# Layer 0 of a two-layer image kernel: gates made with tanh and spread over the slots, and a context that lags behind the attention

## The chip, the cores and the metric

The kernel runs on one core of one Trainium2 chip. The metric is the device time of one execution in microseconds (us), the median of several executions. A core has five engines that each work through their own list of instructions in order and meet at semaphores: TensorE (PE, with PEld for its weight loads), VectorE (DVE), ScalarE (ACT), GpSimd (POOL) and SyncE (SP), which here only issues DMA transfers.

## The reference, cut to what matters

Layer 0 is linear attention on eight images of 128 x 128 points and 128 channels; layer 1 is a selective scan on its output. Layer 0, and the part of layer 1 that this kernel computes together with it:

```python
q, k, v = split(x @ w_qkv)                     # 4 heads of 32
q = softmax(q over the 32 of a head) * 32**-0.5
k = softmax(k over all 16384 points)
context = einsum('bhdn,bhen->bhde', k, v)
out = (context applied to q) @ w_out + b_out
x1 = layernorm(out) * gamma + beta + x         # layer 0's output
xz = x1 @ Win;  xb, z = split(xz)              # layer 1 begins
zf = silu(z)                                   # "the gates", used at the very end of layer 1
```

## The kernel before, in words

The program is three parts one after the other: `layer0`, `layer1_front` and `layer1_scan`. Only `layer0` is touched.

**Tiling.** An image lies in SBUF channel by channel as `xs[b % 2]` (`x` in the profile), 128 partitions by 16384 points, so two images are held at a time. It is worked in 32 groups of 512 points (`NG`, `GN`). Images are taken in the order `ORDER`; `b` below is the place in that order, 0 to 7.

**Stages of one group.** Context: `key` (matmul `pk`, copy to `k`), `larger` (running maximum over four groups, folded to 128 columns), `fold` (transpose `pmt`, maximum `m` per partition, the scale `a`, a diagonal `dg`), `spread` (the maximum to all partitions, `pmx`), `value` (`pv`, copied to `vt`), `subtract` and `raise_to` (exponential), `add` (four matmuls into `pc`). Attention: `query` (matmul `pq`, maximum `qm`, difference `q`, both on DVE), `exponent` (exp on ACT), `normalize` (sum, reciprocal, product on POOL), `through_wo` (four matmuls `pg`, copy `gt` on ACT), `through_context` (matmul `po`, bias `o` on DVE, square `sq` on ACT), `variance` (DVE), `scale` (three POOL operations that end in `d`), `turn` (four matmuls `pt`), `finish` (`x1t` on ACT, the sum back into `x` on POOL, and for half of the images the store of x1). Gates: `gate_group` makes `z` of a finished group: for some images a copy `v` of the group in the other order of points (DVE, line 152; it is also what is stored as x1 for `ORDER[b] < 4`), then for each of two channel halves a matmul `pz` (line 161), Silu on ACT (line 163) and a store to `zs`.

**Loops.** `image(b)` runs slots `t`. In a slot the attention of image b takes group t (its later stages take t-1, t-2, t-3), and the context of image b+1 takes group `a = t - later` with `later = 1`, its `value` and exponential five groups behind, its `add` six. An image has 39 slots; the first call, `b = -1`, has only a context. The gates of image b-1 are all made in slot 0 of image b, 32 groups in a row, and then image b+1 is loaded over the buffer of image b-1. The last image has no context; there two gate groups are made in each slot, one of image 6 and one of image 7.

**What sets the order.** The code is written slot by slot and `in_order` pins every engine to the order in which the code issues: an instruction that waits holds all that stand behind it on its engine. PSUM tiles of the tag `ps` rotate through six banks, so a matmul waits until the sixth tile before its own has been read. SP issues the DMAs in program order.

```python
for t in range(later + NG + BK + 2):
    a = t - later
    ...
    at(through_wo, t - 1)
    ...
    at(exponent, t)
```

Of the kernel before, what the change touches and what calls it, by code (L numbers as in the profile page):

```python
# [8 lines left out]
F32 = mybir.dt.float32  # L9
BF16 = mybir.dt.bfloat16  # L10
AF = mybir.ActivationFunctionType
ALU = mybir.AluOpType
AX = mybir.AxisListType
# [3 lines left out]
P = 128  # L17
B = 8
# [3 lines left out]
NC2 = 2  # L22
R = 8
K = 4
GW = 4
GN = GW * H
NG = W // GW
BK = 4
ORDER = (0, 1, 4, 5, 2, 3, 6, 7)
LATER = 1  # L30
CH = 1024
CW = CH // H
NCH = L // CH
# [44 lines left out]
def layer0(ctx: ExitStack, tc, xT, w_qkv, w_out, b_out, gamma, beta, win, x1, zs):  # L78
# [12 lines left out]
    nc = tc.nc  # L91
    const = ctx.enter_context(tc.tile_pool(name="l0c", bufs=1))
    wp = ctx.enter_context(tc.tile_pool(name="l0w", bufs=2))
    sm = ctx.enter_context(tc.tile_pool(name="l0s", bufs=4))
    ps = ctx.enter_context(tc.tile_pool(name="l0p", bufs=6, space=PSUM))
    psc = ctx.enter_context(tc.tile_pool(name="l0pc", bufs=1, space=PSUM))

    ident = const.tile([P, P], F32, name="ident")
# [7 lines left out]
    nc.sync.dma_start(wq, w_qkv)  # L106
    wz = const.tile([P, NC2 * P], F32, name="wz")
    nc.sync.dma_start(wz, win[:, NC2 * P :])
    wo = const.tile([P, P], F32, name="wo")
    nc.sync.dma_start(wo, w_out)  # L110
    bb = const.tile([P, GW, P], F32, name="bb")
# [13 lines left out]
    xs = [const.tile([P, W, H], F32, name=f"x{i}") for i in range(2)]  # L125
# [13 lines left out]
    def group(b, g):  # L139
        return xs[b % 2][:, g * GW : (g + 1) * GW, :]  # L140

    def load(b, pieces=range(8)):
        for i in pieces:
            s = slice(16 * i, 16 * i + 16)
            nc.sync.dma_start(xs[b % 2][:, s, :], xT[ORDER[b], :, s, :])

    def gate_group(b, g):

        v = group(b, g)
        if ORDER[b] % K < 2 or ORDER[b] < B // 2:  # L150
            t = wp.tile([P, GW, P], F32, name="v", bufs=4)
            nc.vector.tensor_copy(
                t, xs[b % 2].rearrange("p w h -> p h w")[:, g * GW : (g + 1) * GW, :]
            )
            if ORDER[b] < B // 2:
                nc.sync.dma_start(x1[ORDER[b]][:, g * GN : g * GN + GN], t.rearrange("p w h -> p (w h)"))
            if ORDER[b] % K < 2:
                v = t
        for c in range(NC2):
            pz = ps.tile([P, GW, P], F32, name="pz", tag="ps")  # L160
            nc.tensor.matmul(pz, wz[:, c * P : c * P + P], v, start=True, stop=True)
            z = wp.tile([P, GW, P], F32, name="z", tag="k", bufs=7)
            nc.scalar.activation(z, pz, AF.Silu)
            dst = zs[ORDER[b], c][:, g * GN : g * GN + GN]
            nc.sync.dma_start(dst, z.rearrange("p w h -> p (w h)"))

    def gate(b):

        for g in range(NG):
            gate_group(b, g)  # L170
        if b + 2 < B:
            load(b + 2)

    def context(b):

        ks, pks, ms, runs, scales = {}, {}, {}, {}, {}

        def key(g):
            pk = ps.tile([P, GW, P], F32, name="pk", tag="ps")
            nc.tensor.matmul(pk, wq[:, P : 2 * P], group(b, g), start=True, stop=True)  # L180
            ks[g] = k = wp.tile([P, GW, P], F32, name="k", tag="k", bufs=7)
            nc.scalar.copy(k, pk)
            pks[g] = pk

        def larger(g):
            pk = pks.pop(g)
            j, i = divmod(g, BK)
            if i == 1:
                runs[j] = run = wp.tile([P, GW, P], F32, name="run")
                nc.vector.tensor_tensor(run, pk, ks[g - 1], ALU.max)  # L190
            elif i > 1:
                nc.vector.tensor_tensor(runs[j], pk, runs[j], ALU.max)

            if i == BK - 1:
                run = runs[j]
                nc.vector.tensor_tensor(run[:, 0:2], run[:, 0:2], run[:, 2:4], ALU.max)
                nc.vector.tensor_tensor(run[:, 0], run[:, 0], run[:, 1], ALU.max)

        def fold(g):

            j, i = divmod(g, BK)
            if i < BK - 1:
                return
            run = runs.pop(j)
            turned = ps.tile([P, P], F32, name="pmt", tag="ps")
            nc.tensor.transpose(turned, run[:, 0, :], ident)
            ms[j] = m = sm.tile([P, 1], F32, name="m")
            nc.vector.tensor_reduce(m, turned, AX.X, ALU.max)
            if j:
                nc.vector.tensor_tensor(m, m, ms[j - 1], ALU.max)  # L210
                scales[j] = a = sm.tile([P, 1], F32, name="a")
                nc.vector.tensor_tensor(a, ms.pop(j - 1), m, ALU.subtract)
            runs[j] = dg = sm.tile([P, P], F32, name="dg", bufs=2)
            nc.vector.tensor_scalar(dg, ident, m, None, ALU.mult)

        def spread(g):
            j, i = divmod(g, BK)
            if i == BK - 1:
                nc.tensor.matmul(pm[:, j % 2, :], ones, runs.pop(j), start=True, stop=True)
                if j:  # L220
                    nc.scalar.activation(scales[j], scales[j], AF.Exp)

        def value(g):
            pv = ps.tile([P, GW, P], F32, name="pv", tag="ps")
            nc.tensor.matmul(pv, wq[:, 2 * P : 3 * P], group(b, g), start=True, stop=True)
            nc.scalar.copy(vts[g % 3][:, :, 0:P], pv)

        def subtract(g):

            mb = pm[:, g // BK % 2 : g // BK % 2 + 1, :]  # L230
            nc.vector.tensor_tensor(ks[g], ks[g], mb.to_broadcast([P, GW, P]), ALU.subtract)

        def raise_to(g):
            nc.scalar.activation(ks[g], ks[g], AF.Exp)

        def add(g):
            k = ks.pop(g)
            j, n = divmod(g, BK)
            for i in range(GW):
                nc.tensor.matmul(  # L240
                    pc, k[:, i, :], vts[g % 3][:, i, :],
                    start=(n == 0 and i == 0), stop=(n == BK - 1 and i == GW - 1),
                )
            if n < BK - 1:
                return
            if j:
                nc.vector.scalar_tensor_tensor(total, total, scales.pop(j), pc, ALU.mult, ALU.add)
            else:
                nc.vector.tensor_copy(total, pc)
            if g == NG - 1:  # L250
                rs = sm.tile([P, 1], F32, name="rs")
                nc.vector.reciprocal(rs, total[:, P : P + 1])
                for h in range(NH):
                    s = slice(HD * h, HD * h + HD)
                    nc.vector.tensor_scalar(
                        ctxs[b % 2][s, s], total[s, s], rs[s, :], HD**-0.5, ALU.mult, ALU.mult
                    )

        return key, larger, fold, spread, value, subtract, raise_to, add

    def attend(b):
# [69 lines left out]

        return query, exponent, normalize, through_wo, through_context, variance, scale, turn, finish

    def image(b):

        key = larger = fold = spread = value = subtract = raise_to = add = None
        query = exponent = normalize = through_wo = through_context = None
        variance = scale = turn = finish = None
        later = LATER if b >= 0 else 0
        if b + 1 < B:  # L340
            key, larger, fold, spread, value, subtract, raise_to, add = context(b + 1)
        if b >= 0:
            (query, exponent, normalize, through_wo, through_context, variance, scale, turn,
             finish) = attend(b)

        def at(stage, g):
            if stage is not None and 0 <= g < NG:
                stage(g)

        for t in range(later + NG + BK + 2):  # L350
            a = t - later
            at(scale, t - 2)
            at(finish, t - 3)
            at(query, t)
            if b == B - 1 and t < NG:
                gate_group(b - 1, t)
            at(through_wo, t - 1)
            if b == B - 1 and 4 <= t < NG + 4:
                gate_group(b, t - 4)
            at(exponent, t)  # L360
            at(subtract, a - BK - 1)
            at(raise_to, a - BK - 1)
            at(key, a)
            at(normalize, t)
            at(fold, a - 1)
            at(value, a - BK - 1)
            at(larger, a)
            at(through_context, t - 1)
            at(add, a - BK - 2)
            at(turn, t - 2)  # L370
            at(spread, a - 1)
            at(variance, t - 1)
            if t == 0 and 0 < b < B - 1:
                gate(b - 1)

    with in_order(tc):
        load(0)
# [892 lines left out]
```

## Time and profile before

| | us |
|---|---|
| median of 3 runs (9255.66 to 9263.38) | 9257.32 |
| the profiled execution | 9261.02 |
| its span | 9259.2 |
| layer 0 ends (the first instruction of the next part) | 2388 |
| first query matmul of images 0 to 7 | 109, 336, 634, 933, 1221, 1507, 1804, 2098 |

The span of the profiled execution is 1.8 us shorter than its time. Of its 9259.2 us layer 0 takes the first 2388, in which TensorE is busy about 90% of the time; from there on VectorE and GpSimd are the full engines. In the profile a float32 matmul shows as two instructions, so the 256 query matmuls are counted as 512. "Idle before, releaser" tells how long an engine stood still ahead of an instruction, and what it waited for.

### The profile page before, as it was taken

The page shows a single profiled execution, that of the slowest core. Times are in us where ns is not written, and L with a number is a line of the kernel's source. Part 1 is how long each engine was busy: PE and PEld are TensorE (multiplying, and loading weights), DVE is VectorE, ACT ScalarE, POOL GpSimd, SP SyncE. Part 2 cuts the span into 40 slices and gives each one's busy share as a digit, 9 for nine tenths or more (in the row PEclk, how much of TensorE's full clock was granted, in tenths as well). Part 3 has the DMA queues.
Part 4 walks back from the last instruction along what each step waited for, and adds up shares of the span by engine and source line. Part 5 has one row for each costly group of instructions (what it writes and reads, how often), then busy time and mean ns, then how long its engine had stood idle before and what let it go on. Part 6 is the DMA issues. An engine that isn't in the chain of part 4 may idle for free. (4 is left out here: it accounts for less than half of the span.)

```text
span 9259.2 us, 91316 instructions
## 1 busy us (share of the span) xinstructions
PE 6337.5 (68%) x24512; PEld 3096.6 (33%) x24512; DVE 7992.0 (86%) x7953; ACT 7099.7 (77%) x8066; POOL 7316.5 (79%) x4684
## 2 busy tenths in 40 slices
PE   8899998988899999999434636446364463643636
PEld 5555555554333333333101304114031140311403
DVE  6667666774699999999799999999999999999996
ACT  5555555657789999999688887887878888888885
POOL 3446444554588988888599899998999989999897
PEclk9999999999999999999655757557575575755857
DMA  1322333123478789888758769587695876957767
GB/s 76 146 84 96 137 121 146 70 109 137 148 242 249 251 246 244 245 246 241 206 154 238 208 185 258 158 230 216 179 260 159 222 225 178 257 165 218 230 174 211
DMA packets 934769, 1750.66 MB, mean 189 GB/s; under 512 B 150228, under 2 KB 376148, under 8 KB 926064
## 3 DMA queue, kind: packets, MB, share of 16 engines
q1 hardware_dynamic: 873328, 1509.92, 49.4%
q0 software_dynamic: 60928, 234.90, 13.8%
q8 instruction: 200, 3.28, 0.1%
q14 instruction: 313, 2.56, 0.1%
HBM read 1052.36 MB, written 692.12 MB: 188 GB/s over the span
## 5 line engine op out<-in xcount | busy, mean ns | idle before, releaser
L951 POOL TENSOR_TENSOR h<-ubt,sp 128x1024 f32<-128x1024 f32 x1024 | 2422.4, 2399 | 348.4 <-ACT mv L1058 124.1
L934 PE MATMUL px<-rows,dtw 128*128 128x512 bf16 x2048 | 953.5, 565 | 2266.2 <-DVE y L1001 1084.5
L534 DVE SCALAR_TENSOR_TENSOR acc<-xb,cw,acc 128x1024 f32<-128x1024 f32 x1024 | 1320.3, 1289 | 133.7 <-ACT xb L502 89.9
L526 POOL TENSOR_TENSOR tap<-tap 128x1024 f32<-128x1024 f32 x512 | 1224.0, 2394 | 243.9 <-ACT tap L524 220.6
L938 ACT ACTIVATE sp<-px 128x1024 f32<-128x1024 f32 x1024 | 1047.3, 1024 | 435.4 <-PE px L934 418.1
L961 DVE TENSOR_TENSOR_SCAN h<-px,h 128x1024 f32<-128x1024 f32 x512 | 1177.3, 2331 | 31.7 <-ACT px L942 15.1
L934 PEld LDWEIGHTS <-dtw 128*128 128x128 bf16 x2048 | 169.1, 110 | 3089.1 <-issue 1022.7
L959 DVE TENSOR_TENSOR_SCAN h<-px,h 128x1024 f32<-128x1024 f32 x512 | 1177.9, 2330 | 21.4 <-POOL h L951 18.8
L1009 POOL TENSOR_TENSOR y<-y,h 128x512 f32<-128x512 f32 x768 | 1159.8, 1559 | 3.8 <-DVE h L982 3.8
L942 ACT ACTIVATE px<-sp,sa 128x1024 f32<-128x1024 f32 x1024 | 1110.4, 1109 | 6.1
L515 PE MATMUL acc<-xi,wt 128*128 128x512 f32 x2048 | 938.3, 601 | 53.7 <-ACT ures L539 53.7
L524 ACT ACTIVATE tap<-xb,cw 128x1024 f32<-128x1024 f32 x768 | 837.3, 1139 | 15.2 <-POOL xb L499 15.1
L282 POOL TENSOR_TENSOR q<-q,qs 128x512 f32<-128x512 f32 x256 | 272.2, 1063 | 695.5 <-DVE qs L281 695.5
L938 ACT ACT_TABLE_LOAD x512 | 656.9, 1283 | 170.0 <-PE px L934 168.0
L942 ACT ACT_TABLE_LOAD x512 | 656.9, 1283 | 9.1
L1074 PEld LDWEIGHTS px<-wg,z 128*128 128x128 f32 x4096 | 575.3, 225 | 114.8 <-issue 109.1
L1074 PE MATMUL px<-wg,z 128*128 128x128 f32 x4096 | 574.7, 308 | 0.0
L967 PE MATMUL pc<-rows,csel 128*128 128x512 bf16 x1024 | 517.5, 586 | 78.2 <-DVE rstd L1062 74.5
L515 PEld LDWEIGHTS acc<-xi,wt 128*128 128x128 f32 x2048 | 375.1, 189 | 574.4 <-issue 411.9
L488 PE MATMUL pxb<-xi,wi 128*128 128x512 f32 x1024 | 496.2, 607 | 2.1 <-ACT xb L497 2.1
L298 ACT ACTIVATE sq<-o 128x512 f32<-128x512 f32 x256 | 161.2, 630 | 421.0 <-DVE o L296 419.8
L1001 DVE TENSOR_TENSOR y<-y,px 128x1024 f32<-128x1024 f32 x384 | 468.6, 1220 | 14.4
(153 smaller groups left out, 15038.8 us busy)
## 6 DMA issues: line engine op xcount, KB each, us to landing
ubt<-ubs SPq DMA_DIRECT2D x1024, 512.0 KB
zs<-z SPq DMA_DIRECT2D x512, 256.0 KB
ubs<-ures SPq DMA_DIRECT2D x256, 512.0 KB
ubs<-turned SPq DMA_DIRECT2D x256, 512.0 KB
z<-zs SPq DMA_DIRECT2D x256, 512.0 KB
y<-gs POOLq DMA_DIRECT2D x128, 1024.0 KB, 10.3
gs<-du POOLq DMA_DIRECT2D x96, 1024.0 KB, 8.6
rows<-xps SPq DMA_DIRECT2D x1536, 60.0 KB
```

The costliest lines, as they stand in the source:

```text
L515: nc.tensor.matmul(acc[:, s, :], wt[:, j, c, :], x, start=(j == 0), stop=(j == len(ON_PE) - 1))
L524: nc.scalar.activation(t, at(n, c, *d), AF.Copy, scale=weight(n, c, *d))
L526: nc.gpsimd.tensor_tensor(sums[n, c], sums[n, c], t, ALU.add)
L534: nc.vector.scalar_tensor_tensor(acc, at(n, c, *d), weight(n, c, *d), acc, ALU.mult, ALU.add)
L934: nc.tensor.matmul(p[:, hf * 512 : hf * 512 + 512], sl.dw[:, c * P : c * P + P], src, start=True, stop=True)
L938: nc.scalar.activation(t, da[n, c], AF.Softplus)
L942: nc.scalar.activation(da[n, c], sp[n, c], AF.Exp, scale=sa[:, sl.s, c : c + 1])
L951: nc.gpsimd.tensor_tensor(h, u, t, ALU.mult)
L959: nc.vector.tensor_tensor_scan(e[:, ::-1], x[:, ::-1], e[:, ::-1], start, ALU.mult, ALU.add)
L961: nc.vector.tensor_tensor_scan(e, x, e, start, ALU.mult, ALU.add)
L1009: nc.gpsimd.tensor_tensor(v[:, c], v[:, c], h[:, c], ALU.add)
L1074: nc.tensor.matmul(po[:, w, :], z[:, c, w * H : w * H + H], wg[:, c, :], start=(c == 0), stop=(c == NC2 - 1))
```

## The change

Gates: Silu is made as half of z times (tanh of half of z, plus one). The weights `wz` are halved once at the start; ACT makes the tanh from PSUM, DVE forms (tanh + 1) times the PSUM tile with one instruction, and the store follows. `gate_group` falls into four stages, `ready` (the copy `v`, now on ACT), `gate_project`, `gate_tanh` and `gate_store`. They are no longer made in one go: a table `plan` gives each slot its gate groups. At the start of image b the gates of image b-1 that are still open are made two to a slot; from slot 35 on, when image b's attention has ended, its own gates are made one to a slot. `ready` runs one slot ahead, at the end of a slot.

Context: it starts when the open gates are done and `LEAD = 2` slots more have passed (`laters[b]`, 1 for image 0 and then 16, 9, 12, 11, 11, 11), so that an image has 39, 54, 47, 50, 49, 49 and 49 slots, and 37 for the last. The load of image b+1 is issued when the last gate of image b-1 has been issued.

Order in the slot: `exponent` comes ahead of `through_wo`; it stood behind it. Fold of maxima: one `tensor_reduce` instead of two `tensor_tensor` maxima; `m` and `a` are made with a scalar operand per partition instead of a second tensor.

```diff
+    nc.vector.tensor_scalar(wz, wz, 0.5, None, ALU.mult)
...
-            nc.vector.tensor_copy(
-                t, xs[b % 2].rearrange("p w h -> p h w")[:, g * GW : (g + 1) * GW, :]
-            )
+            nc.scalar.copy(t, xs[b % 2].rearrange("p w h -> p h w")[:, g * GW : (g + 1) * GW, :])
...
-            z = wp.tile([P, GW, P], F32, name="z", tag="k", bufs=7)
-            nc.scalar.activation(z, pz, AF.Silu)
...
+    def gate_tanh(b, g, c):
+        zts[b, g, c] = z = wp.tile([P, GW, P], F32, name="z", bufs=4)
+        nc.scalar.activation(z, pzs[b, g, c], AF.Tanh)
+
+    def gate_store(b, g, c):
+
+        z = zts.pop((b, g, c))
+        nc.vector.scalar_tensor_tensor(z, z, 1.0, pzs.pop((b, g, c)), ALU.add, ALU.mult)
+        nc.sync.dma_start(zs[ORDER[b], c][:, g * GN : g * GN + GN], z.rearrange("p w h -> p (w h)"))
...
-                nc.vector.tensor_tensor(run[:, 0:2], run[:, 0:2], run[:, 2:4], ALU.max)
-                nc.vector.tensor_tensor(run[:, 0], run[:, 0], run[:, 1], ALU.max)
+                runs[j] = top = sm.tile([P, P], F32, name="top", bufs=2)
+                nc.vector.tensor_reduce(top, run.rearrange("p w h -> p h w"), AX.X, ALU.max)
...
-                nc.vector.tensor_tensor(m, m, ms[j - 1], ALU.max)
+                nc.vector.tensor_scalar(m, m, ms[j - 1], None, ALU.max)
...
-                nc.vector.tensor_tensor(a, ms.pop(j - 1), m, ALU.subtract)
+                nc.vector.tensor_scalar(a, ms.pop(j - 1), m, None, ALU.subtract)
...
+    for b in range(-1, B):
+        left = NG - done[b - 1] if b > 0 else 0
+        if b >= 0:
+            laters[b] = -(-left // 2) + LEAD if left else 1
+        for t in range(laters[b] + NG + BK + 2 if b < B - 1 else NG + 5):
+            gates = plan[b, t] = []
+            for _ in range(2 if b < B - 1 else 1):
+                if b > 0 and done[b - 1] < NG:
+                    gates.append((b - 1, done[b - 1]))
+                    done[b - 1] += 1
+                    if done[b - 1] == NG and b + 1 < B:
+                        loads[b, t] = b + 1
+            if b < B - 1:
+                own = b >= 0 and not gates and t > NG + 2
+            else:
+                own = done[b] <= t - 5
+            if own and done[b] < NG:
+                gates.append((b, done[b]))
+                done[b] += 1
...
-        for t in range(later + NG + BK + 2):
-            a = t - later
+        for t in (t for i, t in times if i == b):
+            a = t - laters[b]
+            first, second = (plan[b, t] + [None, None])[:2]
             at(scale, t - 2)
             at(finish, t - 3)
             at(query, t)
-            if b == B - 1 and t < NG:
-                gate_group(b - 1, t)
+            if first:
+                gate_project(*first)
+                gate_tanh(*first, 0)
+            at(exponent, t)
+            if first:
+                gate_tanh(*first, 1)
+                gate_store(*first, 0)
             at(through_wo, t - 1)
-            if b == B - 1 and 4 <= t < NG + 4:
-                gate_group(b, t - 4)
-            at(exponent, t)
+            if second:
+                gate_project(*second)
             at(subtract, a - BK - 1)
             at(raise_to, a - BK - 1)
             at(key, a)
             at(normalize, t)
+            if first:
+                gate_store(*first, 1)
+            if second:
+                for c in range(NC2):
+                    gate_tanh(*second, c)
             at(fold, a - 1)
             at(value, a - BK - 1)
             at(larger, a)
             at(through_context, t - 1)
+            if second:
+                for c in range(NC2):
+                    gate_store(*second, c)
             at(add, a - BK - 2)
             at(turn, t - 2)
             at(spread, a - 1)
             at(variance, t - 1)
-            if t == 0 and 0 < b < B - 1:
-                gate(b - 1)
+            for g in plan.get(then.get((b, t)), ()):
+                ready(*g)
+            if (b, t) in loads:
+                load(loads[b, t])
```

More of the change, by code (lines that the diff above doesn't have):

```diff
@@ L29 @@
 ORDER = (0, 1, 4, 5, 2, 3, 6, 7)
-LATER = 1
+LEAD = 2
 CH = 1024
@@ L145, in load, with ready @@
             nc.sync.dma_start(xs[b % 2][:, s, :], xT[ORDER[b], :, s, :])
-    def gate_group(b, g):
+    vs, pzs, zts = {}, {}, {}
+    def ready(b, g):
         v = group(b, g)
@@ L158, in gate_group, with gate_project @@
                 v = t
+        vs[b, g] = v
+    def gate_project(b, g):
+        v = vs.pop((b, g))
         for c in range(NC2):
-            pz = ps.tile([P, GW, P], F32, name="pz", tag="ps")
+            pzs[b, g, c] = pz = ps.tile([P, GW, P], F32, name="pz", tag="ps")
             nc.tensor.matmul(pz, wz[:, c * P : c * P + P], v, start=True, stop=True)
-            z = wp.tile([P, GW, P], F32, name="z", tag="k", bufs=7)
[L163 to L172, printed above, removed]
+    def gate_tanh(b, g, c):
[5 more added lines that the diff above has]
+        nc.sync.dma_start(zs[ORDER[b], c][:, g * GN : g * GN + GN], z.rearrange("p w h -> p (w h)"))
     def context(b):
@@ L180, in key @@
             nc.tensor.matmul(pk, wq[:, P : 2 * P], group(b, g), start=True, stop=True)
-            ks[g] = k = wp.tile([P, GW, P], F32, name="k", tag="k", bufs=7)
+            ks[g] = k = wp.tile([P, GW, P], F32, name="k", bufs=7)
             nc.scalar.copy(k, pk)
@@ L203, in fold @@
                 return
-            run = runs.pop(j)
+            top = runs.pop(j)
             turned = ps.tile([P, P], F32, name="pmt", tag="ps")
-            nc.tensor.transpose(turned, run[:, 0, :], ident)
+            nc.tensor.transpose(turned, top, ident)
             ms[j] = m = sm.tile([P, 1], F32, name="m")
@@ L332, in attend @@
         return query, exponent, normalize, through_wo, through_context, variance, scale, turn, finish
+    plan, laters, loads = {}, {-1: 0}, {}
+    done = [0] * B
+    for b in range(-1, B):
[17 more added lines that the diff above has]
+                done[b] += 1
+    assert done == [NG] * B
+    times = list(plan)
+    then = dict(zip(times, times[1:]))
     def image(b):
@@ L338, in image @@
         variance = scale = turn = finish = None
-        later = LATER if b >= 0 else 0
         if b + 1 < B:
```

## The prediction

> **What bounds the kernel now.** I first took the windows, busy time per engine in stretches of 50 us (columns: window, length, PE, PEld, DVE, ACT, POOL busy with counts, granted clock, DMA share, GB/s).
>
> ```profile
> 200.00:250.00 50.00, 47.96 (x250) 32.60 (x248) 42.10 (x73) 31.13 (x55) 35.66 (x39) 1.00 0.00 1
> 350.00:400.00 50.00, 48.29 (x104) 18.06 (x102) 17.94 (x25) 31.02 (x52) 0.00 (x0) 1.00 1.01 382
> 2200.00:2250.00 50.00, 42.98 (x165) 22.88 (x166) 19.81 (x35) 40.15 (x58) 25.10 (x28) 1.00 0.42 158
> ```
>
> TensorE is full while attention and context run together (first line), full and DMA-bound in the gate run of slot 0 (second), less full in the last image (third). Then the timeline of one slot (start, duration, engine, line):
>
> ```profile
> 204.12 1.02 PE L268 MATMUL pq<-x,wq 128*128 128x512 f32 x2
> 204.98 1.05 PE L288 MATMUL pg<-wo,q 128*128 128x128 f32 x8
> 205.87 1.02 PE L180 MATMUL pk<-x,wq 128*128 128x512 f32 x2
> 206.73 1.02 PE L225 MATMUL pv<-x,wq 128*128 128x512 f32 x2
> 207.59 1.02 PE L294 MATMUL po<-gt,ctxn 128*128 128x512 f32 x2
> ...
> 210.23 1.02 PE L268 MATMUL pq<-x,wq 128*128 128x512 f32 x2
> ...
> 206.25 0.69 DVE L272 TENSOR_TENSOR q<-pq,qm 128x512 f32<-128x512 f32 x1
> ...
> 206.12 0.59 ACT L290 COPY gt<-pg 128x512 f32<-128x512 f32 x1 [0.62 <-PE pg L288]
> 206.98 0.63 ACT L275 ACTIVATE q<-q 128x512 f32<-128x512 f32 x1 [0.27 <-DVE q L272]
> ```
>
> Matmul groups follow at 0.86 (four-fold ones 0.89), seven make 6.11, and po stands 3.47 after pq. gt comes before the exponential; keep that in mind. Every fourth slot (fold) takes 7.82: VectorE is held there, as the group view over 130:2100 (POOL at work) and over 20:100 (POOL idle) says:
>
> ```profile
> L212 DVE TENSOR_TENSOR a<-m 128x1 f32<-128x1 f32 x49 | 41.9, 854 | 1.7
> L212 DVE TENSOR_TENSOR a<-m 128x1 f32<-128x1 f32 x6 | 1.0, 159 | 0.2
> ```
>
> Image boundary, the last slot of the layer, and the rows for the changed operations (ACT's only strided copy of 512 elements is layer 1's `turned`):
>
> ```profile
> 336.36 1.02 PE L268 MATMUL pq<-x,wq 128*128 128x512 f32 x2
> 341.52 3.51 DVE L152 COPY v<-x 128x512 f32<-128x512 f32 x4
> 406.15 1.02 PE L268 MATMUL pq<-x,wq 128*128 128x512 f32 x2
> 416.82 2.04 PE L180 MATMUL pk<-x,wq 128*128 128x512 f32 x2 [8.75 <-DMA x<-in_x]
> 2370.65 2.07 PE L288 MATMUL pg<-wo,q 128*128 128x128 f32 x8 [3.12 <-POOL q L282]
> L163 ACT ACT_TABLE_LOAD x32 | 41.1, 1283 | 1.1 <-PE pz L161 0.5
> L606 ACT COPY turned<-ures x101: 1036/1087/1943, 2675.0 to 4484.1; 128x512 f32<-128x512 f32 x96, 128x1024 f32<-128x1024 f32 x5
> ```
>
> Slot 0 takes 69.8, and slot 1 14.2, most of it a wait for the load. 32 gates are 64 matmuls of 0.86 = 55 of pure TensorE time, so about 21 of these 84 are lost at a boundary, beside a 27.2 tail of seven context slots. Image 7 runs 8.69 a slot where its matmuls need 6.94.
>
> **What the Trainium skill says.** "ScalarE: Activation LUTs", Table sets: exp and tanh share a set, and each switch loads a table; the trace has 2 x 32 loads of 1.283 in image 7. "SBUF — State Buffer", Who interferes with whom: a DVE operation with two SBUF inputs, or in a two-port mode, and a GpSimd one block each other; the 854 against 159 ns agree. "TensorE: Matmul & The Clock Gate", Part 1: an idle TensorE drops to half clock; pg above took 2.07 in place of 1.05 after 3.12 idle.
>
> **The change part by part.** All of layer 0; pure matmul time is the same before and after, so what counts is the period of each kind of slot.
>
> *Fold.* m and a at 0.16 each (the idle-POOL rows; at worst the old 0.46 and 0.85) cut the wait for dg of about 1.1; a fold then costs its two matmuls, +0.23 on a stalled slot. The one maximum over 512 elements (0.69, as the other reductions) replaces 1.09 + 0.38; both stand beside TensorE work.
>
> *Exponent ahead of gt (S, attention and context).* pq ends at 1.02, qm starts at 1.06, q at 1.83, ends at 2.5; exp 2.55, gt 3.14 to 3.72, po at 3.78 instead of 3.47, and 0.1 for its weight load that no longer hides (po waiting for gt in image 7: 0.96 to the next group instead of 0.86). S = 6.53; with fold 6.76. That eats the fold's gain: four slots 26.35 against 26.15. Between 6.11 (hidden) and 6.9 (DVE late by the 0.3 seen in this slot).
>
> *Attention alone, or with keys only (A).* The loop var, qm, q, exp, gt, po, o, sq, var: 0.60+0.78+0.73+0.59+0.59+0.06+1.13+0.04+0.78+0.65 = 5.95, as now (5.5 to 5.9).
>
> *Two gates and attention (G).* TensorE 6.94. But ACT now runs two copies `ready` behind sq: gt 0.59, to po 0.06, po 1.13, o 0.72, to sq 0.1, then sq 0.58, copies 2 x 1.02, x1t 0.72, tanh 0.55, exp 0.59, tanh 0.55, and 0.05 of handover: 7.68. Without copies (images 6, 7) TensorE's 6.97. The tanh needs no table load and costs what Silu does (0.60). DVE's products (0.69, as other 512-element operations with PSUM; four are 2.8) fit: its slot is 6.5. PSUM: pz is now read twice, but a's bank is needed by pt, c's by the next slot's second pz, after the products.
>
> *Own gates beside the context (C).* The copy v is ACT's last instruction in a slot, and the first matmul of the next slot waits for it where v feeds pz (images 0 to 3); pk, pv and pc are queued behind. Loop: to pz 0.08, pz 1.13, to tanh 0.06; tanh and product to the subtraction 1.25, subtraction 0.72, exp 0.59, k and vt copies 1.08, v 1.06: 5.97, TensorE 4.33. Without keys 5.43 (3.47). Images 4, 5, where v is only stored: ACT's 4.66 and 4.12. Image 6: 4.4 and 3.5.
>
> *Boundaries.* The load has two A slots to land (before: 6.3 from issue to the first key), so its wait goes. DMA per G slot 1.5 MB, half the 382 GB/s of the burst; SP issues six transfers of about 0.6. The wz product at the start hides behind the 15.4 wait for the first load. Draining slots 32 to 34: 12.2 (11.3 in image 0), last context slot 2.8, first gate slots 5.3 cheaper (pipeline empty); the odd last gate slot (images 2, 4) 6.6. Five key-only slots with a fold 30.4, two lead slots 11.9: 42.3.
>
> Sums (before: 109, then 227, 298, 299, 288, 286, 297, 294, 290):
> 0: 11.5 + 30.4 + 26 x 6.53 + 1.4 + 11.3 + 3 x 5.43 + 2.8 = 243
> 1: 14 G 102 + 42.3 + 11 S 72 + 12 + 13 x 5.97 + 5 x 5.43 + 2.8 = 337
> 2: 47 + 42.3 + 18 S 118 + 12 + 6 x 5.97 + 30 = 286
> 3: 10 G 71.5 + 42.3 + 15 S 99 + 12 + 9 x 5.97 + 30 = 308
> 4: 63 + 42.3 + 16 S 105 + 12 + 8 x 4.66 + 5 x 4.12 + 2.8 = 283; 5: 284; 6: 278
> 7: five one-gate slots 30, 13 x 6.97, 13 one-gate slots x 6.5 (A's loop plus a tanh), 22.5 from the last query to the end (29.1 now) = 227
>
> With 109: 2357 (before rounding) against 2388, 31 less. Little, since image 1 pays 39 for 19 own gates behind the copy, while image 7, with 14 gates fewer and no table loads, saves 63. The parts after layer 0 keep their instructions. 9261 - 31 = 9230 for the profiled execution; the median stands 3.7 below it: 9226.
>
> **The rivals.**
> *Chains hidden.* If copies and products hide, G falls to 6.94 (57 slots, 42), own-gate slots to TensorE's (28 x 1.64 + 18 x 1.96 + 16 x 0.33 + 10 x 0.65 = 93): 9226 - 135 = 9091. For it: every engine's sum is below TensorE's in G. Against: the order on ACT, and 1.04 to 1.09 for such a copy.
> *The order costs more (S).* If VectorE stays 0.3 late, as in the slot shown, S is 6.9: 118 x 0.37 = 44 more, 9270. It ends slower than before from S = 6.8. Against: a longer slot gives VectorE time to catch up.
> *Half clock.* In the 50 own-gate slots of images 0 to 3 TensorE idles 1.6 of 6; if it drops to half there, 4.33 becomes 8.7: +2.7 x 50 = 135, 9361, decided from 12 such slots. For it: the 2.07 above. Against: image 7 idles 1.75 of 8.69 at clock 1.00.
> *Tables.* If tanh and exp did not share a table, about 185 slots would load two: 2.57 x 185 = 475, mostly on ACT's loops; 9700. The skill speaks against it.
>
> **How the numbers follow.** Forecast 0.45 (own range 9200 to 9250), hidden 0.22, dearer order 0.20, half clock 0.08, tables 0.03; 0.02 for others. What this kernel can tell from no change is about 0.2%, 18.5 us: 9239 to 9276. Faster: 0.22, and 0.85 of the forecast's 0.45, 0.60. Same: 0.07 from the forecast and half of the dearer order, 0.17. Slower: the rest, 0.23. The range, 9100 to 9300, takes in the dearer order and most of the hidden case (9091 plus what S or a copy may still cost); outside are its lower edge (0.09), the clock and the tables.
>
> **What would show it.** Right: query to query 6.5 in full slots, with po waiting for gt; own-gate slots of images 1 to 3 near 6 with pz waiting for ACT's v; G near 7.7 with ACT unbroken behind sq; one table load in layer 0; a at 0.16; no load wait at the first key; layer 0 ends near 2357. Wrong: slots at 6.1, copies of 0.6, a clock below 1.00 in own-gate stretches.

## The result: 24 us slower, where 31 us faster were forecast

| | before | changed | forecast |
|---|---|---|---|
| median of nine runs each | 9256.67 | 9280.91 | 9226 |
| the profiled execution | 9261.02 | 9274.46 | 9230 |
| layer 0 ends (first instruction of the next part) | 2388.2 | 2398.5 | 2357 |
| first load of the next part issued | 2391.3 | 2408.2 | – |
| from there to the end of the span | 6867.9 | 6864.5 | – |

The ratio of changed to before is 1.0027, 95% interval 1.0017 to 1.0037: slower, by little more than can be told from no change. The two profiled executions differ by 13.4, of which layer 0 is 10.3, the handover to the next part 6.6, and the rest -3.4. (The profiled run of before was 4.4 above its median, that of the changed kernel 6.5 below its own, which is why the medians stand 24 apart.)

The windows of the changed kernel, columns as before:

```profile
200.00:250.00 50.00, 47.59 (x240) 30.62 (x239) 38.43 (x71) 30.69 (x56) 34.98 (x39) 1.00 0.00 1
400.00:450.00 50.00, 45.68 (x180) 25.43 (x179) 36.28 (x63) 39.60 (x62) 28.41 (x32) 1.00 0.53 200
600.00:650.00 50.00, 40.76 (x148) 22.49 (x147) 25.69 (x45) 33.03 (x55) 0.00 (x0) 1.00 0.38 142
2200.00:2250.00 50.00, 49.38 (x198) 28.78 (x199) 40.94 (x71) 32.13 (x58) 32.88 (x38) 1.00 0.48 185
```

Attention with context (first line) does 240 matmul instructions in 50 us where it did 250. Two gates a slot (second) use half of the DMA share of the old burst and leave TensorE 4 us of 50 idle, own gates with context (third) leave 9. The last image (fourth) is full, where it had 7 us idle.

Next, the timeline of image 0, the slot in which the maximum over four groups is folded, and the slot after it (start, duration, engine, line, operation, idle before and its releaser):

```profile
217.46 1.02 PE L272 MATMUL pq<-x,wq 128*128 128x512 f32 x2
...
221.20 1.13 PE L298 MATMUL po<-gt,ctxn 128*128 128x512 f32 x2
...
222.18 0.69 DVE L196 TENSOR_TENSOR run<-pk,run 128x512 f32<-128x512 f32 x1 [0.51 <-ACT k L186]
222.91 1.05 DVE L201 TENSOR_REDUCE top<-run 128x128 f32<-128x512 f32 x1
223.88 0.68 DVE L300 TENSOR_TENSOR o<-po,bb 128x512 f32<-128x512 f32 x1
223.94 1.02 PE L272 MATMUL pq<-x,wq 128*128 128x512 f32 x2
...
225.92 0.68 DVE L274 TENSOR_REDUCE qm<-pq 128x16 f32<-128x512 f32 x1
226.70 0.69 DVE L276 TENSOR_TENSOR q<-pq,qm 128x512 f32<-128x512 f32 x1
227.43 0.63 ACT L279 ACTIVATE q<-q 128x512 f32<-128x512 f32 x1 [1.48 <-DVE q L276]
227.96 0.57 ACT L294 COPY gt<-pg 128x512 f32<-128x512 f32 x1
228.58 1.13 PE L298 MATMUL po<-gt,ctxn 128*128 128x512 f32 x2 [0.89 <-ACT gt L294]
...
231.55 1.02 PE L272 MATMUL pq<-x,wq 128*128 128x512 f32 x2
```

The first slot takes 6.48, the second 7.61 (7.60 is the usual length). In the first, po stands 3.74 behind pq; in the second 4.64. Read backwards from there: po waits for gt, gt stands behind the exponential, and the exponential waits for q, which starts 2.76 behind pq where it started 1.86 behind it in the first slot. The delay comes from `top`, which held VectorE: `o` could start only at 223.88, while po had been finished since 222.33, and `sq`, the variance, qm and q follow `o` one after the other.

In the kernel before, such a pair of slots took 6.11 and 7.82:

```profile
210.23 1.02 PE L268 MATMUL pq<-x,wq 128*128 128x512 f32 x2
...
216.34 1.02 PE L268 MATMUL pq<-x,wq 128*128 128x512 f32 x2
...
224.16 1.02 PE L268 MATMUL pq<-x,wq 128*128 128x512 f32 x2
```

The timeline over own gates of image 1, which feed the matmul from the copy v:

```profile
618.66 1.07 ACT L155 COPY v<-x 128x512 f32<-128x512 f32 x1
619.78 1.98 PE L166 MATMUL pz<-v,wz 128*128 128x512 f32 x4 [1.12 <-ACT v L155]
...
624.37 1.08 ACT L155 COPY v<-x 128x512 f32<-128x512 f32 x1
625.50 1.98 PE L166 MATMUL pz<-v,wz 128*128 128x512 f32 x4 [1.12 <-ACT v L155]
```

The same view over two gates a slot, in the same image:

```profile
420.21 1.99 PE L166 MATMUL pz<-v,wz 128*128 128x512 f32 x4 [0.73 <-ACT v L155]
422.03 1.05 PE L292 MATMUL pg<-wo,q 128*128 128x128 f32 x8
422.92 1.88 PE L166 MATMUL pz<-v,wz 128*128 128x512 f32 x4
424.64 1.02 PE L298 MATMUL po<-gt,ctxn 128*128 128x512 f32 x2
426.48 0.63 ACT L302 ACTIVATE sq<-o 128x512 f32<-128x512 f32 x1 [1.05 <-DVE o L300]
427.02 2.02 ACT L155 COPY v<-x 128x512 f32<-128x512 f32 x2
428.12 1.13 PE L166 MATMUL pz<-v,wz 128*128 128x512 f32 x2 [0.71 <-ACT v L155]
```

The own-gate slot is 5.72 from pz to pz, and 1.12 of it is TensorE waiting for v. The two-gate slot is 7.91: a copy of v releases the first pz, both gates and pg follow, po comes behind the second gate, and only then `o`, `sq` and the next copy. Finally the groups that answer to those shown of before (count | busy us, mean ns | idle ahead). ACT's over layer 0:

```profile
L155 ACT COPY v<-x 128x512 f32<-128x512 f32 x192 | 200.0, 1071 | 0.0
L186 ACT ACT_TABLE_LOAD x1 | 1.3, 1283 | 0.7 <-PEq L1302 0.7
```

And VectorE's of the fold over 160:320, with POOL at work:

```profile
L201 DVE TENSOR_REDUCE top<-run 128x128 f32<-128x512 f32 x6 | 6.3, 1049 | 0.2
L216 DVE TENSOR_SCALAR a<-m 128x1 f32<-128x1 f32 x6 | 1.3, 215 | 0.2
```

The copy costs 1.07, where 1.06 was forecast. ACT loads one table where it loaded 78 in layer 0, as the Trainium skill, "ScalarE: Activation LUTs", Table sets, has it for tanh and exp. The scale takes 0.21 where it took 0.854 beside POOL (0.16 was forecast, from the old form with POOL idle). The reduction takes 1.05, not 0.69.

### The profile page after: what moved, and what is told of

Its sections match the earlier page's. It is cut to its first block, busy times and chain, and to the rows that moved or that the text cites. A ratio compares the mean times of both kernels' runs of the same rounds, so it can differ in the third digit from the quotient of the medians.

```text
span 9272.7 us, 92100 instructions
## 1 busy us (share of the span) xinstructions
PE 6289.4 (68%) x24350; PEld 3088.6 (33%) x24512; DVE 8109.0 (87%) x8210; ACT 7157.2 (77%) x8182; POOL 7315.6 (79%) x4684
## 5 line engine op out<-in xcount | busy, mean ns | idle before, releaser
L977 PE MATMUL px<-rows,dtw 128*128 128x512 bf16 x1893 | 909.4, 573 | 2300.3 <-DVE y L1044 1052.1
L175 DVE SCALAR_TENSOR_TENSOR z<-z,pz 128x512 f32<-128x512 f32 x512 | 343.1, 683 | 220.9 <-ACT z L170 220.1
```

The costliest lines, as they stand in the source:

```text
L977: nc.tensor.matmul(p[:, hf * 512 : hf * 512 + 512], sl.dw[:, c * P : c * P + P], src, start=True, stop=True)
```

## Where the forecast's sum and the trace part

Image by image, from first query to first query:

| image | forecast | measured | miss |
|---|---|---|---|
| start | 109 | 112.1 | +3 |
| 0 | 243 | 246.0 | +3 |
| 1 | 337 | 342.5 | +6 |
| 2 | 286 | 294.1 | +8 |
| 3 | 308 | 313.3 | +5 |
| 4 | 283 | 291.0 | +8 |
| 5 | 284 | 287.7 | +4 |
| 6 | 278 | 286.1 | +8 |
| 7 | 227 | 225.7 | -1 |

And by kind of slot, forecast to measured: full slot 6.53 to 6.48; slot after a maximum 6.76 to 7.60; attention alone 5.95 to 5.88; two gates where v feeds pz 7.68 to 7.92; two gates without a copy (in the last image) 6.97 to 6.94; one gate 6.5 to 6.37; own gates from a copy 5.97 to 5.72. Twenty-four slots after a maximum are 24 x 0.84 = 20, and with the first full slots (7.19) and the slots with keys only the misses of this kind come to about 31. A slip in the sum took 6 of them back: the 11.5 at the head of image 0 was read from the kernel before, where it spans slots 0 and 1 (both queries are issued together at 109.39 and the next at 120.86), and slot 1 is then counted again among the five slots with keys only. That leaves 25. The two-gate stages are 19 over (5.7, 4.3, 4.7, 4.8, 0.1 and -0.7 in images 1 to 6), the start 2.7, the tails -4, the last image -1.4: 41 in all. With 6.6 at the handover and -3.4 after it, this is the 44 by which the profiled execution missed its 9230.

## Experiments

In each, "before" is the kernel before as it ran in the same job, and a ratio is to its median there: 9258.55 for the exponential moved in either kernel, the old fold and the copy two slots ahead; 9255.22 for the fold alone, both edits, the copy on GpSimd and tanh; 9258.87 for the shorter reduction and the one slot of lead.

**The exponential back behind gt.** One line of the changed kernel is moved.

```diff
-            at(exponent, t)
             if first:
                 gate_tanh(*first, 1)
                 gate_store(*first, 0)
             at(through_wo, t - 1)
+            at(exponent, t)
```

> The changed kernel with the exponential put back behind the copy gt. Theory 1 (the order on ScalarE costs in every full slot): plain slots of attention and context fall from 6.48 to 6.11, fold slots from 7.60 to about 6.5, attention-only slots from 5.88 to 5.5; some 85 us less than the changed kernel, near 9196, and faster than the kernel before. Theory 2 (the matmul po would wait for something else anyway, a PSUM bank or VectorE): slots stay at 6.4 to 6.5, less than 20 us.

Measured: 9178.31, ratio 0.9917 (0.9902 to 0.9932), 103 less than the changed kernel. The same two slots of image 0 in this run's timeline:

```profile
214.31 1.06 DVE L201 TENSOR_REDUCE top<-run 128x128 f32<-128x512 f32 x1
215.39 1.02 PE L272 MATMUL pq<-x,wq 128*128 128x512 f32 x2
217.40 0.58 ACT L294 COPY gt<-pg 128x512 f32<-128x512 f32 x1
218.84 0.63 ACT L279 ACTIVATE q<-q 128x512 f32<-128x512 f32 x1 [0.86 <-DVE q L276]
218.97 1.02 PE L298 MATMUL po<-gt,ctxn 128*128 128x512 f32 x2
...
221.84 1.02 PE L272 MATMUL pq<-x,wq 128*128 128x512 f32 x2
```

The reduction is as long, and the exponential starts as late: 3.45 behind pq, where it was 3.49. But gt has gone ahead of it, po stands 3.58 behind pq, and the slot takes 6.45: 6.11 and 0.34 for the fold, whose two extra matmuls were forecast at 0.23. Full slots are 6.11, attention alone or with keys mostly 5.05 to 5.65. Only two-gate slots lose by it: 7.97 for 7.92 where v feeds pz, 7.47 for 7.22 where it is only stored.

**The old fold in the changed kernel.**

```diff
-                runs[j] = top = sm.tile([P, P], F32, name="top", bufs=2)
-                nc.vector.tensor_reduce(top, run.rearrange("p w h -> p h w"), AX.X, ALU.max)
+                nc.vector.tensor_tensor(run[:, 0:2], run[:, 0:2], run[:, 2:4], ALU.max)
+                nc.vector.tensor_tensor(run[:, 0], run[:, 0], run[:, 1], ALU.max)
...
-                nc.vector.tensor_scalar(m, m, ms[j - 1], None, ALU.max)
+                nc.vector.tensor_tensor(m, m, ms[j - 1], ALU.max)
...
-                nc.vector.tensor_scalar(a, ms.pop(j - 1), m, None, ALU.subtract)
+                nc.vector.tensor_tensor(a, ms.pop(j - 1), m, ALU.subtract)
```

> The changed kernel with the whole fold of maxima as it was: two maxima of two tensors, m and a made from two tensors. Theory 1 (the strided reduction of 1.05 us holds VectorE no longer than the two maxima did; the fold slot is long because o comes late): fold slots grow from 7.60 to 8.0 to 8.5, 15 to 40 us more than the changed kernel. Theory 2 (the new reduction is what makes the fold slot 7.60 where 6.76 was forecast): fold slots shrink, 20 us less.

Measured: 9284.16, ratio 1.0029 (1.0017 to 1.0040), the same as the changed kernel's 1.0027, so neither theory held. The slot after a maximum takes 7.42 and the one after that 6.76, against 7.60 and 6.48. So with the exponential ahead of gt the fold's form is worth nothing, whichever it is: the two maxima (0.54 and 0.29 here) hold VectorE less than `top` in the slot of the maximum, and the old m and a (0.50 and 0.97 against 0.21 each) hold it more in the slot after.

**The fold alone, in the kernel before** (the same diff read the other way).

> The kernel before with the new fold of maxima alone: one reduction, m and a with scalar operands. Theory 1 (the fold itself pays where gt stands ahead of the exponential): fold slots fall from 7.82 to 6.45, 70 us less than the kernel before, near 9188. Theory 2 (the strided reduction of 1.05 makes o late whatever the order): fold slots stay above 7.2, less than 30 us.

Measured: 9191.74, ratio 0.9927 (0.9911 to 0.9944), 63 faster; the slot after a maximum falls from 7.82 to 6.45. This edit is worth 63 us with the old order and nothing with the new one.

**The exponential ahead of gt, in the kernel before.**

```diff
+            at(exponent, t)
             at(through_wo, t - 1)
...
-            at(exponent, t)
```

> The kernel before with the exponential ahead of the copy gt, and nothing else changed. Theory 1: plain slots of attention and context grow from 6.11 to 6.5, attention with keys only from 5.5 to 5.9, and the kernel becomes slower by 40 to 80 us. Theory 2 (hidden in the kernel before): no change.

Measured: 9292.27, ratio 1.0040 (1.0025 to 1.0055), 34 slower. Full slots are 6.49, those after a maximum 7.42 and 6.76. Image 7 gains (8.69 to 7.74 in most of its slots, 24 in all), so the order costs the rest of layer 0 about 58.

Four successive slots with one maximum, side by side, say what these runs have in common:

| kernel | fold | exponential | the four slots | sum |
|---|---|---|---|---|
| before | old | behind gt | 7.82, 3 x 6.11 | 26.15 |
| before, fold alone | new | behind gt | 6.45, 3 x 6.11 | 24.78 |
| before, exponential moved | old | ahead | 7.42, 6.76, 2 x 6.49 | 27.16 |
| changed | new | ahead | 7.60, 3 x 6.48 | 27.04 |
| changed, exponential back | new | behind gt | 6.45, 3 x 6.11 | 24.78 |
| changed, old fold | old | ahead | 7.42, 6.76, 2 x 6.49 | 27.16 |

The sum goes by the place of the exponential. The fold's form counts only where the exponential stands behind gt.

**A shorter reduction.** This takes four neighbouring points, and so another maximum than the reference's groups; it is a size test.

```diff
-                nc.vector.tensor_reduce(top, run.rearrange("p w h -> p h w"), AX.X, ALU.max)
+                nc.vector.tensor_reduce(
+                    top, run.rearrange("p w h -> p (w h)").rearrange("p (a b) -> p a b", b=GW), AX.X, ALU.max
+                )
```

> The changed kernel, but the reduction of maxima reads four adjacent points for each result instead of four points 128 apart: as many elements, another set of maxima, so the stabilising maximum is not the one that the reference's softmax needs. If the stride is why it takes 1.05 and not the 0.69 of other reductions of 512, it takes 0.69 here; if VectorE's delay in the slot of the maximum is what makes the next slot 7.60 (theory 1), that slot shrinks by the same 0.36, to about 7.25. If the fold slot is long for another reason (theory 2: the wait for dg or a PSUM bank), it stays at 7.6.

Measured in the profiled execution alone: 9254.45, 20 below that of the changed kernel. All instances of the reduction (count: shortest, median, longest in ns):

```profile
L201 DVE TENSOR_REDUCE top<-run x64: 685/686/687, 22.4 to 2128.7; 128x128 f32<-128x512 f32 x64
```

The same 512 elements in order take 0.686, which is the duration that the forecast used, and the slot after a maximum falls from 7.60 to 7.24. So the stride cost 0.36 in each such slot, one for one; it is not the whole 0.84.

**The copy v two slots ahead.** It is issued one slot earlier, and own gates begin one slot later, since the group must be finished when it is copied.

```diff
-                own = b >= 0 and not gates and t > NG + 2
+                own = b >= 0 and not gates and t > NG + 3
...
-            for g in plan.get(then.get((b, t)), ()):
+            for g in plan.get(then.get(then.get((b, t))), ()):
```

> The changed kernel with the copy v made two slots ahead instead of one, and own gates from slot 36 on, so that pz never waits for a copy just issued. Theory 1 (pz stands behind the copy at the end of the slot): own-gate slots of images 1 to 3 fall from 5.72 to 4.7, slots with two gates there from 7.92 to 7.2; some 67 us less, near 9214. Theory 2 (ScalarE's load is the bound, wherever the copy stands): less than 15 us.

Measured: 9204.06, ratio 0.9944 (0.9929 to 0.9959), 77 less than the changed kernel. The stretch from the last query of an image to the next image's first, which holds its own gates, is 102.7, 66.5 and 84.6 in images 1 to 3 where it was 123.3, 84.0 and 100.4 (image 2 has one own gate fewer here). Own-gate slots of image 1 fall from 5.72 to 4.33, which is TensorE's own time; two-gate slots take 7.22 in all images where they took 7.92 in images 1 to 4. The wait of pz for v was a real part of both stages.

**Both edits.** The exponential behind gt and the copy two slots ahead, together.

> The changed kernel with both repairs: the exponential behind gt and the copy v two slots ahead. If the two costs are separate (theory 1), own-gate slots of images 1 to 3 go to 4.7 (49 us less than with the exponential alone) and slots with two gates there from 7.97 to 7.5 (15 less): near 9114. If they share a cover (theory 2), 9150 or more.

Measured: 9105.04, ratio 0.9836 (0.9821 to 0.9850). Against the changed kernel it is 176 less, where the two edits gave 103 and 77 singly: they add. Two-gate slots are 7.48 here, so with both edits this stage is the one that the late exponential still hurts.

**The copy on GpSimd, and the exponential ahead only where there are gates.**

```diff
-            nc.scalar.copy(t, xs[b % 2].rearrange("p w h -> p h w")[:, g * GW : (g + 1) * GW, :])
+            nc.gpsimd.tensor_copy(t, xs[b % 2].rearrange("p w h -> p h w")[:, g * GW : (g + 1) * GW, :])
...
-            at(exponent, t)
             if first:
+                at(exponent, t)
                 gate_tanh(*first, 1)
                 gate_store(*first, 0)
             at(through_wo, t - 1)
+            if not first:
+                at(exponent, t)
```

with the two-slot lines of above.

> As the kernel with both repairs, but the copy v made by GpSimd and not by ScalarE, and the exponential ahead of gt only in slots that make gates. Theory 1 (ScalarE's loop with two copies bounds the slots with two gates): they fall from about 7.5 to TensorE's 6.95, own-gate slots from 4.7 to 4.4: some 40 us less than with both repairs, near 9075. Theory 2 (GpSimd, at 6.7 of work in such a slot, [...]becomes the bound): two-gate slots stay at 7.2 or more, no gain.

Measured: 9082.16, ratio 0.9812 (0.9797 to 0.9826), 23 less than with both edits, where 40 were expected. The windows over two-gate slots and over own gates with context:

```profile
350.00:400.00 50.00, 50.00 (x205) 29.41 (x205) 41.89 (x72) 32.79 (x58) 47.05 (x51) 1.00 0.60 227
550.00:600.00 50.00, 50.00 (x191) 28.23 (x190) 32.35 (x58) 31.67 (x60) 14.42 (x14) 1.00 0.46 173
```

TensorE is busy for all of both stretches, two-gate slots are 6.94 and own gates 4.33 apart: this is the "chains hidden" rival of the prediction (6.94 and 4.33). The 4.33 was there already with the copy two slots ahead on ACT. The 6.94 is the work of the other engine: two-gate slots of this kernel differ from those of the run with the copy two slots ahead (7.22) in the engine of the copy alone. A copy takes much the same there:

```profile
L155 POOL COPY v<-x x192: 1052/1089/1122, 322.2 to 1746.2; 128x512 f32<-128x512 f32 x192
```

**The same with one slot of lead in place of two** (`LEAD = 1`).

> As the kernel with the copy on GpSimd and both repairs, but LEAD = 1: the context starts one slot earlier. An attention-only slot uses 3.5 of its 5.05 on TensorE, so six of them left out save about 9 us (near 9073), if the load still lands within one slot (6.3 us from issue to first key in the kernel before). If it doesn't, the first key waits up to 5 us at each of six images and nothing is gained.

Measured: 9059.30, ratio 0.9782 (0.9765 to 0.9798), the fastest of all, 199.6 below before. The first load of the next part is issued at 2190.6 instead of 2203.1, so layer 0 explains 12.5 (9 were expected) of the 23 between the medians; the rest lies in the parts behind it, which this edit does not touch, and stays open.

**The gates by tanh in the kernel before,** still in one go in slot 0.

```diff
+    nc.vector.tensor_scalar(wz, wz, 0.5, None, ALU.mult)
...
-            nc.scalar.activation(z, pz, AF.Silu)
+            nc.scalar.activation(z, pz, AF.Tanh)
+            nc.vector.scalar_tensor_tensor(z, z, 1.0, pz, ALU.add, ALU.mult)
```

> The kernel before with gates by tanh and a VectorE product, everything else as it was. Theory 1: the 64 table loads of the last image go, its slots fall from 8.69 to about 7.0, the runs of gates in slot 0 stay bound by DMA and TensorE: 50 us less than the kernel before, near 9207. Theory 2 (PSUM banks held longer by the product stall pz): the gate runs of slot 0 grow by 5 or more each and the gain is under 20.

Measured: 9626.72, ratio 1.0401 (1.0386 to 1.0417), 371 slower, where 50 faster were expected. Image 7 gains as intended (8.69 to 6.94 a slot), and the two gate runs in which v does not feed pz stay near 62 (62.7 and 63.5, from 61.9 and 61.6). The other four go from 62 to 70 up to 171 to 175. The timeline of the first of them:

```profile
358.13 0.73 DVE L153 COPY v<-x 128x512 f32<-128x512 f32 x1
358.91 2.92 PE L162 MATMUL pz<-v,wz 128*128 128x512 f32 x4 [2.11 <-DVE v L153]
...
362.49 0.69 DVE L165 SCALAR_TENSOR_TENSOR z<-z,pz 128x512 f32<-128x512 f32 x1 [0.96 <-ACT z L164]
363.10 0.72 DVE L153 COPY v<-x 128x512 f32<-128x512 f32 x1
```

And the window over 50 us of it (columns as before, the granted clock ahead of the last two):

```profile
350.00:400.00 50.00, 30.47 (x38) 8.74 (x36) 19.19 (x29) 11.49 (x20) 0.00 (x0) 0.64 0.38 145
```

On VectorE the next group's copy now stands behind this group's products, so copy, pz, tanh, product and copy follow one another, and TensorE waits 2.1 for each group. In that idling its granted clock is 0.64 (1.00 in the same window of the kernel before). In the first such run (341:516) the waits of pz for v sum to 68.7, and the rest of the 174.7, 106, is nearly twice the 55 that the 64 matmuls take at full clock. Theory 2 expected gate runs to grow through PSUM banks; those without v in front of pz did not, so it is the copy behind the products that costs. Tanh with the copy on the same engine is a loss of 371. Whether the split into stages or the copy on another engine is what makes it usable in the changed kernel, no run separates.

## Why the prediction was wrong, point by point

**The failed step is "Fold", with "Two gates and attention" close behind.** In the account above they are 20 and 19 of the 44; the handover, which the sum left out, is 6.6. "Fold" said that a fold "then costs its two matmuls, +0.23 on a stalled slot", and of the maximum over 512 elements that it takes 0.69 and stands "beside TensorE work". Measured is 1.05 and +1.12. Two things were wrong in it. The duration was taken from reductions that read in order; this one reads with a stride of 128 elements, and the run with neighbouring points prices that at 0.36 a slot. The larger error, the other 0.53 of the 0.89, was the cover. It holds with the exponential behind gt: both kernels with the new fold and that order show 6.45, the forecast's own "+0.23" plus 0.11. But the same text moved the exponential, and with that a late VectorE goes straight through the exponential and gt to po. The two edits were priced each against the kernel before, and their sum was taken; the table of four slots shows that they do not add (63 us of gain in one order, nothing in the other).

**"Exponent ahead of gt" was right where VectorE is on time**: 6.53 to 6.48, with po 3.74 behind pq where 3.78 was worked out. The rival "the order costs more" had the right mechanism, a late VectorE, at the wrong place: not 0.3 in every slot, but the whole of 1.12 in one slot of four. That its 9270 is nearer to the result than the forecast is chance: it took 0.37 in 118 slots, and had no part of the 19 in the gate stages.

**"Two gates and attention" took the wrong loop.** ScalarE's own instructions were summed to 7.68. The loop measured is v to pz, pz, pg, pz, pz, po, `o`, `sq`, copy: 1.82 to pg, 0.89, 1.72 to po, 1.06 to `o`, 0.78, 0.54 to the copies, and 1.10 for the first one and its handover, 7.91. What was left out is that the second gate's matmuls stand ahead of po on TensorE, while the copies behind `sq` on ACT feed the next gate. Where the copy is only stored (images 5 and 6) that loop is open, and the slot takes 7.22. The first three gate slots of an image (4.47, 7.58 and 8.74 in image 1) are 3 cheaper than three others, where 5.3 was taken.

**"Own gates" and "attention alone" were right**: pz waits for ACT's v, and 5.72 and 5.88 against 5.97 and 5.95 are a little better than forecast. That a chain, and not TensorE, sets them is shown for own gates by the copy two slots ahead (4.33), for attention alone by the exponential back behind gt (5.05).

**"Boundaries" were right inside the layer** (no wait for a load at the first key, tails 4 better) **and looked at too little behind it.** The sum ended with the layer; the next part's start was taken to follow at the same distance. The trace shows 9.7 from the layer's end to the first load of the next part, where it was 3.1. In time order, on VectorE, POOL and SyncE's queue:

```profile
2400.20 5.88 DVE L464 CAST ident<-ident 128x128 bf16<-128x128 f32 x1
2400.31 6.16 SPq L176 DMA_DIRECT2D zs<-z  x2
2400.33 5.75 DVE L175 SCALAR_TENSOR_TENSOR z<-z,pz 128x512 f32<-128x512 f32 x1
2400.95 4.43 POOL L496 MEMSET xb<- 128x5200 f32 x1
2408.21 1.02 SPq L524 DMA_DIRECT2D xi<-x  x2
```

A type conversion of the next part comes ahead of the last gate product, and both are recorded as lasting to 2406.08, 0.7 after the end of POOL's memset; the last gate store waits for the product, and the load stands behind the store. Before, a gate ended on ACT and no such product existed, so that the same slow conversion held no store:

```profile
2389.68 6.05 DVE L421 CAST ident<-ident 128x128 bf16<-128x128 f32 x1 [1.33 <-POOL ident masks.py:199]
2391.30 1.02 SPq L481 DMA_DIRECT2D xi<-x  x2
```

The tanh run tells the conversion and the product apart. It has both, but its last product comes ahead of the conversion:

```profile
2756.38 0.69 DVE L165 SCALAR_TENSOR_TENSOR z<-z,pz 128x512 f32<-128x512 f32 x1 [0.17 <-ACT z L164]
2758.26 6.05 DVE L423 CAST ident<-ident 128x128 bf16<-128x128 f32 x1 [1.11 <-POOL ident masks.py:199]
2760.27 1.02 SPq L483 DMA_DIRECT2D xi<-x  x2
```

There the next part starts at 2756.75 and the load follows 3.5 later, while in all eight kernels with the gates in stages, whose last product stands behind the conversion, it follows 9.7 later. So it is the product behind the conversion that delays the load. Why the conversion takes so long is not shown: the Trainium skill, "SBUF — State Buffer", Who interferes with whom, says that a cast on VectorE can run in a mode in which it and a GpSimd instruction exclude each other for a whole instruction, which fits 6.05 beside a memset of 4.43, but no run has the conversion without the memset.

**The last image was right**: 225.7 for 227, slots of 6.94, one table load. **The clock rival** did not happen in the changed kernel: 1.00 with TensorE idle for 9 of 50 us. It did in the tanh run above, at 0.64, where it idled more.

**Why so little came out of so much.** With the new fold in both, and the exponential behind gt in both, the kernel before has 0.9927 and the changed one 0.9917: the spread of the gates, tanh and the lag together bring about 9 us, and the two intervals overlap (0.9911 to 0.9944, 0.9902 to 0.9932). What they win at the boundaries and in image 7 (64 there) is paid back, in large part in slots that wait for the copy v. With the copy two slots ahead they bring a further 75 (0.9836), and on GpSimd with one slot of lead 0.9782.

## What to carry to other kernels

Before an instruction is moved ahead of another on an in-order engine, ask which engine feeds it and how late that engine is in its worst slot, not its usual one: here one move turned one late slot in four from nearly free (6.45 for 6.11) into the most expensive (7.60 for 6.48). Price edits of one change together, each with the others made, because a cover that one edit relies on can be what another takes away. Here a copy that feeds a matmul did best two slots ahead of it, on the engine with the most idle time.

## What was not expected of the hardware

A maximum on VectorE over 512 float32 elements takes 1.05 with a stride of 128 elements between those compared, and 0.686 with neighbours; POOL at work or idle makes little difference (1.049 and 1.029). A copy with such a stride on the reading side takes 1.07 on ACT and 1.09 on GpSimd; gt, which ACT reads in order, but from PSUM, takes 0.57 to 0.59. TensorE, kept waiting 2.1 us ahead of every group of four matmul instructions, was granted 0.64 of its clock over 50 us, while 1.12 of waiting in each slot of 5.7 left it at 1.00.
